# Two attention chunks per window: one set of scores in six PSUM banks, and whole output and query groups taking turns in two

## The chip, the cores and the metric

The kernel runs on one core of one Trainium2 chip. The metric is the device time of one execution in microseconds; three runs of the kernel before gave 1732.31, 1732.99 and 1734.68, a median of 1732.99.

The engines are named as the profile names them: PE is TensorE (matmuls; PEld is its weight loads), DVE is VectorE, ACT is ScalarE, POOL is GpSimd, and SP is SyncE, which issues nearly all DMAs here. Each engine works through its own list of instructions in order. [...]

## The reference, cut to what matters

Thirty-two batches of 512 query rows of 640 numbers attend to 77 context rows with 20 heads of 32 numbers. Only the text part of the original block is there, since the context has 77 rows and no more.

```
q = x @ to_q_w;  k = ctx @ to_k_w;  v = ctx @ to_v_w          # 640 wide, heads of 32
p = softmax(q k^T / sqrt(32))                                  # per head: 512 x 77
out = merge_heads(p v) @ to_out_w + to_out_b + x               # 32 x 512 x 640, float32
```

Everything is float32. Products that need more precision than one pass gives are made of a high and a low part in three passes, `(0,0), (0,1), (1,0)` of weights and data.

## The kernel before, in words

A first stage, which the change leaves alone, computes keys and values of all batches from the context and stores them in DRAM. It ends at about 250 us. The main loop then goes through 160 chunks: chunk n is one fifth of batch n // 5, that is 128 columns, or four heads (HPC = 4), of all 512 query rows, which make four tiles (NQ = 4) of 128.

For a chunk the steps are these:

- `queries(n)`: 15 matmuls (five parts of 128 input columns, three passes) into a PSUM bank of the kind `pq`. `copy_q` brings the bank to SBUF as `qt`.
- `scores(n)`: 16 matmuls of 77 columns, each recorded twice, one for each head and tile. The four heads sit in four row groups of TensorE and write four banks of the kind `sc`.
- `maxima(n)`: DVE takes the negative row maximum of each head's four tiles at once. `exps(n, i)`: ACT computes the exponentials of head i in four instructions, each with its sum, into `pn` (two buffers, by n mod 2).
- `normalize(n)`: DVE's reciprocal and POOL's multiplication in place. `transpose_p(n)`: DVE transposes 32x32 blocks of `pn` into `z` (two buffers).
- `move_p(n)`: four DMAs bring `z` into a `raw` buffer, of which there are two, with the keys on the partitions.
- `values(n)`: four matmuls (eight records) of `raw` and the batch's values into a bank of the kind `pa`. `high_a` (ACT) and `low_a` (DVE) split the result into a high and a low part, `at`. Ten such tiles live at a time.
- `group(b, c, ks)`: once all five chunks of batch b are there, the output projection of 128 columns, 15 matmuls into a bank `po`. `turn` (DVE) transposes it, and `add` (POOL) adds it to `ys[b]`, which holds x of the batch and gets the bias from `bias_of` (POOL). `store_y` writes it out with four DMAs.

The batch's x arrives through `load_x` (four DMAs, one for each quarter of the partitions), is transposed on DVE by `transpose_x` and split by `split_x` (ACT high, POOL low) into five `xt` tiles, of which seven live at a time. x and y buffers are taken in turn from three large ones (`natural`). So a `load_x` can have to wait until the stores from the buffer that it gets have landed.

The order of the work on each engine is written out by hand (`manual_schedule`): it is the order of the calls in `slot(n)`, lines 646 to 741, which runs once for each chunk. In the steady part, TensorE's order in a slot is: scores of n, nine matmuls of an output group, the 15 queries of n + 1, and the other six of the group. In every second slot the values of chunks n - 3 and n - 2 follow. DMAs on SP go out in the order of the code as well, and each issue first waits until its buffer is free and its data is there.

The last batch is handled in `end()`, where the output projection has rows on the partitions (`project`, `finish`).

## Time and profile before

| | |
|---|---|
| Median of three runs | 1732.99 us |
| The profiled execution's own time | 1730.84 us |
| Its span, first to last instruction | 1728.6 us |
| Granted TensorE clock, mean | 0.998 |
| PE busy | 1720.0 us, 100% |
| ACT busy | 1129.0 us, 65% |
| POOL busy | 987.1 us, 57% |
| DVE busy | 974.6 us, 56% |
| DMA bytes moved | 306.50 MB, 177 GB/s in the mean |

The page gives the busy time of each engine, the chain of work that ended last, and the costliest groups of instructions with their line, count and mean length. Other views of the same trace give the instructions of a stretch in order of time (start, length, line, and the idle time ahead of it with what ended it), the busy share of every engine in a stretch with the granted TensorE clock (1.00 is full speed) and the DMA engines' busy share, and for DMAs the time from the issue to the landing. `PE sc L455` is TensorE working on the tile `sc` in line 455. Times of a row are microseconds from the start of the span.

### The profile page before, as it was taken

Reading aid. Unit: us, or ns where it says so; the run is one execution under the profiler, and the core shown is the slowest. Engines: PE = TensorE matmul, PEld = TensorE weight load, DVE = VectorE, ACT = ScalarE, POOL = GpSimd, SP = SyncE. Lnnn points to the kernel's source line nnn. Section 1 sums busy time; section 2 is a strip of 40 time slices with the busy share of each in tenths; the row PEclk is TensorE's granted clock in tenths of the full one; section 3 lists DMA queues with packets and bytes.
Section 4 is the critical chain, followed back from the end, with each engine's and each line's share of the span. In section 5 each row is a group of like instructions: output and inputs, shape, how many; then the busy total and the mean of one; then the engine's idle time right before and its main releaser. Section 6 shows DMA issues by size and latency. Waiting matters only on the chain.

```text
span 1728.6 us, 36822 instructions
## 1 busy us (share of the span) xinstructions
PE 1720.0 (100%) x12460; PEld 1313.9 (76%) x12460; DVE 974.6 (56%) x1559; ACT 1129.0 (65%) x5698; POOL 987.1 (57%) x663
## 2 busy tenths in 40 slices
PE   9999999999999999999999999999999999999999
PEld 7888898677777777777777777777777777777777
DVE  5342235656666566665665666656666566665653
ACT  3131126777777777777777777777777777777771
POOL 1000026666666666666666666666666666666665
PEclk9999999999999999999999999999999999999999
DMA  9847565969888878887888888888878787888775
GB/s 186 163 88 183 115 134 146 214 152 207 177 190 176 189 177 192 189 197 176 192 191 175 193 184 184 184 182 185 195 174 200 166 196 179 192 176 189 176 169 160
DMA packets 363851, 306.50 MB, mean 177 GB/s; under 512 B 88784, under 2 KB 292112, under 8 KB 363664
## 3 DMA queue, kind: packets, MB, share of 16 engines
q1 hardware_dynamic: 360864, 296.61, 77.9%
q0 software_dynamic: 2704, 7.38, 1.4%
q8 instruction: 99, 1.62, 0.4%
q14 instruction: 88, 0.72, 0.1%
q10 hardware_dynamic: 96, 0.16, 0.0%
HBM read 120.36 MB, written 57.88 MB: 103 GB/s over the span
## 4 chain that ended last, share of the span: by engine, by line
PE 96%; DMA 2%; DVE 1%; SPq 1%; issue 0%; ACT 0%; POOL 0%; DVEq 0%; POOLq 0%; ACTq 0%
PE po L568 32%; PE pq L433 31%; PE sc L455 10%; PE pa L515 8%; PE pv L182 7%; PE pk L182 7%; DMA raw<-z 1%; PE po L600 1%; DMA wraw<-in_L_xattn_to_k_w_dram 1%; SPq L99 0%; DVE z L496 0%; DMA cs<-in_ctx_dram 0%; SPq L149 0%; DVE wk_s L90 0%; ACT wk_s L89 0%
## 5 line engine op out<-in xcount | busy, mean ns | idle before, releaser
L477 ACT ACTIVATE pn<-sc,nm 128x77 f32<-128x77 f32 x2560 | 788.6, 364 | 229.7 <-DVE nm L467 228.0
L489 POOL TENSOR_TENSOR pn<-pn,rs 128x1232 f32<-128x1232 f32 x160 | 363.4, 2271 | 478.8 <-DVE rs L487 474.1
L477 ACT ACTIVATION_READ_ACCUMULATOR pn<-sc,nm 128x1 f32 x2560 | 627.2, 245 | 0.0
L568 PE MATMUL po<-at,wo_s 128*128 128x512 f32 x2325 | 598.7, 398 | 0.0
L433 PE MATMUL pq<-xt,wq_s 128*128 128x512 f32 x2355 | 562.7, 390 | 0.0
L433 PEld LDWEIGHTS pq<-xt,wq_s 128*128 128x128 f32 x2355 | 442.3, 188 | 93.6
L568 PEld LDWEIGHTS po<-at,wo_s 128*128 128x128 f32 x2325 | 424.4, 188 | 97.6 <-DVE ot L578 0.8
L467 DVE TENSOR_REDUCE nm<-sc 128x4 f32<-128x308 f32 x640 | 261.1, 470 | 72.1 <-PE sc L455 72.1
L496 DVE STREAM_TRANSPOSE z<-pn 128x1536 f32<-128x1536 f32 x160 | 282.7, 1767 | 4.9 <-DMA raw<-z 3.0
L455 PEld LDWEIGHTS sc<-kb,qt 32*128 32x128 f32 x5120 | 158.1, 187 | 97.8 <-ACT at L529 63.7
L259 POOL TENSOR_TENSOR xt<-xs,xt 128x512 fp32r<-128x512 f32 x157 | 197.8, 1285 | 35.8 <-ACT xt L258 35.8
L578 DVE STREAM_TRANSPOSE ot<-po 128x512 f32<-128x512 f32 x155 | 111.1, 716 | 184.2 <-PE po L568 184.2
L582 POOL TENSOR_TENSOR xs<-xs,ot 128x512 f32<-128x512 f32 x155 | 200.2, 1292 | 2.3 <-DVE ot L578 2.1
L549 POOL TENSOR_TENSOR xs<-xs,bias_y 128x640 f32<-128x640 f32 x124 | 193.0, 1567 | 7.3
L455 PE MATMUL sc<-kb,qt 32*128 32x77 f32 x5120 | 181.8, 278 | 2.2 <-DVE qt L442 2.2
L529 ACT CAST at<-pa 128x512 fp32r<-128x512 f32 x160 | 94.3, 589 | 134.6 <-PE pa L515 134.6
L487 DVE RECIPROCAL rs<-sm 128x16 f32<-128x16 f32 x160 | 40.4, 252 | 219.6 <-ACT pn L477 219.6
L515 PE MATMUL pa<-raw,vb 96*32 96x512 f32 x1280 | 154.9, 599 | 1.3 <-DMA raw<-z 0.9
L534 DVE TENSOR_TENSOR at<-pa,at 128x512 fp32r<-128x512 f32 x160 | 109.6, 685 | 79.1 <-ACT at L529 79.1
L182 PE MATMUL pv<-ct,wv_s 128*128 128x512 f32 (+1 forms) x600 | 134.2, 382 | 0.0
L182 PE MATMUL pk<-ct,wk_s 128*128 128x512 f32 (+1 forms) x600 | 133.8, 382 | 0.3 <-ACT wk_s L89 0.2
L182 PEld LDWEIGHTS pk<-ct,wk_s 128*128 128x128 f32 x600 | 112.1, 188 | 20.2 <-ACT wk_s L89 0.8
(44 smaller groups left out, 698.2 us busy)
## 6 DMA issues: line engine op xcount, KB each, us to landing
raw<-z SPq DMA_DIRECT2D x640, 192.0 KB, 4.1
xs<-in_x_dram SPq DMA_DIRECT2D x256, 320.0 KB, 6.3
out_dram<-xs SPq DMA_DIRECT2D x127, 320.0 KB, 5.0
vb<-v_dram SPq DMA_DIRECT2D x32, 240.0 KB, 6.3
kb<-k_dram SPq DMA_DIRECT2D x32, 192.5 KB, 6.4
cs<-in_ctx_dram SPq DMA_DIRECT2D x12, 512.0 KB, 9.3
k_dram<-ks POOLq DMA_DIRECT2D x20, 256.0 KB, 2.5
v_dram<-vs SPq DMA_DIRECT2D x80, 64.0 KB, 2.3
```

The costliest lines, as they stand in the source:

```text
L182: nc.tensor.matmul(held[j][:, :gn], w[:, k, a, :], cts[g, k][:, c, :gn], start=(k == 0 and n == 0), stop=(k == NK - 1 and n == 2),)
L259: low.tensor_tensor(parts[1], src, parts[0].bitcast(F32), ALU.subtract)
L433: nc.tensor.matmul(pqs[n], wq_s[:, k, a, j * P : (j + 1) * P], xts[b, k][:, c, :], start=(k == 0 and m == 0), stop=(k == NC_ - 1 and m == 2),)
L455: nc.tensor.matmul(sc[:, t, :NKEY], qt[r, t * P : (t + 1) * P], kbs[b % 2][r, j, :], start=True, stop=True, tile_position=(i * HD, 0),)
L467: nc.vector.tensor_reduce(nms[n][:, i], sc[:, :, :NKEY], AX.X, ALU.max, negate=True)
L477: nc.scalar.activation(pnb[n % 2][:, at, :NKEY], sc[:, t, :NKEY], AF.Exp, bias=nms[n][:, i, t : t + 1], accum_out=sms[n][:, at : at + 1],)
L489: nc.gpsimd.tensor_tensor(pf, pf, rs.unsqueeze(2).to_broadcast([P, NQ * HPC, NKEY]), ALU.mult)
L496: nc.vector.transpose(z.rearrange("p c h t j -> p (h t) c j"), pn.rearrange("p a (c i) -> p a c i", i=Q),)
L515: nc.tensor.matmul(pas[n][i * HD : (i + 1) * HD, :].rearrange("p (a q) -> p a q", q=P), vb[:, i, :], raw[:, :, i, :], start=True, stop=Tru ...
L549: nc.gpsimd.tensor_tensor(part, part, biases[1].unsqueeze(1).to_broadcast([P, 4, U]), ALU.add)
L568: nc.tensor.matmul(pos[b, c], wos[0][:, k, a, c * P : (c + 1) * P], ats[b * NC_ + k][:, d, :], start=(k == 0 and m == 0), stop=(k == NC_ - ...
L582: nc.gpsimd.tensor_tensor(part, part, ots.pop((b, c)).rearrange("p (a i) -> p a i", i=Q), ALU.add)
```

## The change

From chunk 8 on, the loop over slots is replaced by a loop over windows of two chunks, n and n + 1, with n even. The work is the same, and its order changes:

- The values of chunks n - 4 and n - 3 come first and go to the banks `po` and `pq`, which output groups and queries use in turn afterwards.
- `scores_of_two` computes the scores of both chunks in one run of 64 records into six banks, the four of kind `sc` and both of kind `pa`. A head's own bank takes six tiles of 80 columns (four of chunk n, two of n + 1), and each of the two other banks takes the remaining two tiles of two heads. Maxima are taken over six tiles for each head, and over two in the shared banks.
- After the scores come a whole output group (15 matmuls), the queries of n + 2, another whole output group, and the queries of n + 3. `qt` has two buffers now. One copy of a window is ACT's, the other DVE's.
- `move_p(n - 2)` and `move_p(n - 1)` are issued in window n, and other DMAs of the window stand between them: with w = n mod 10 these are values, keys, two quarters of x and four of y for w = 0; values and four quarters of x for w = 4; keys and four of y for w = 6; four stores of y and two quarters of x for w = 8. For w = 2 four stores follow the second move.
- Bias additions, x splits and x transposes are dealt out to windows by w.
- In the fill (chunks 0 to 7) chunk 6 joins those whose probability transpose stands behind the query copy, and slot 7 computes the queries of chunks 8 and 9. In the end, two more output groups of the last but one batch are computed inside the last window (`closing`).

```diff
+    def scores_of_two(n):
+        banks = [bank("sc") for _ in range(HPC)] + [bank("pa") for _ in range(2)]
+        views = [
+            sc[:, : s * W].rearrange("p (s k) -> p s k", s=s)[:, :, :NKEY]
+            for sc, s in zip(banks, (6, 6, 6, 6, 4, 4))
+        ]
...
+        last = [(n + 1, 2), (n + 1, 3)]
+        rest = [(n, t) for t in range(NQ)] + [(n + 1, 0), (n + 1, 1)]
+        for step in range(2 * NQ):
+            for i in range(HPC):
+                m, t = (rest + last if i % 2 else last + rest)[step]
+                score(scs[m, i, t], m, i, t)
+            if step == 1:
+                for i in (0, 2):
+                    maxima_of(shared[i], i, 6)
+        return views, shared
...
+    def window(n):
+        w, b = n % 10, n // 10 * 2
+        first, ahead = n == FIRST, n + 2 < N
+        taken = (n - 3,) if first else (n - 4, n - 3)
+        early, later = (divmod(n - FIRST + i, NC_) for i in range(2))
+        for m in taken:
+            values(m, "pq" if m == n - 3 else "po")
+        for m in taken:
+            high_a(m)
+        while held:
+            low_a(held.pop())
+        normalize(n - 1)
+        for m in taken[:-1]:
+            low_a(m)
+        views, shared = scores_of_two(n)
+        low_a(n - 3)
+        for i in range(3):
+            maxima_of(views[i], i)
+        transpose_p(n - 1)
+        maxima_of(views[3], 3)
+        if not first:
+            move_p(n - 2)
+        if w == 0:
+            load_values(b)
+            load_keys(b + 1)
+            load_x(b + 1, (2, 3))
+            load_y(b - 1, range(4))
+        if w == 4:
+            load_values(b + 1)
+            if b + 2 < B:
+                load_x(b + 2)
+        if w == 6:
+            if b + 2 < B:
+                load_keys(b + 2)
+            load_y(b, range(4))
+        if w == 8:
+            if b:
+                store_y(b - 1, range(4))
+            if b + 3 < B:
+                load_x(b + 3, (0, 1))
...
+        for i in range(HPC):
+            exps(n, i)
+        group(*early, range(NC_))
+        turn(*early)
+        for i in (1, 3):
+            maxima_of(shared[i], i, 6)
+        add(*early)
+        move_p(n - 1)
+        if w == 2 and b > 1:
+            store_y(b - 2, range(4))
+        if ahead:
+            queries(n + 2)
+        normalize(n)
+        for i in (0, 2):
+            exps(n + 1, i, range(2, NQ))
+        if ahead:
+            copy_q(n + 2)
...
+        transpose_p(n)
+        for i in (1, 3):
+            exps(n + 1, i, range(2, NQ))
+        for i in (1, 3, 0, 2):
...
+            exps(n + 1, i, range(2))
...
+        if ahead:
+            group(*later, range(NC_))
+            turn(*later)
+            add(*later)
+            queries(n + 3)
+            copy_q(n + 3, nc.vector.tensor_copy)
...
-    for n in range(LATE, N):
+    for n in range(LATE, FIRST):
         slot(n)
+    for n in range(FIRST, N, 2):
+        window(n)
     end()
```

More of the change, by code (lines that the diff above doesn't have):

```diff
@@ L390 @@
     late = []
-    raws, ats, sms, pqs, pas, xrs, pos, scs, nms = ({} for _ in range(9))
+    raws, ats, sms, pqs, pas, xrs, pos, scs = ({} for _ in range(8))
     main.tile([P, HPC * NQ], F32, name="align")
@@ L402 @@
         pnb.append(pn)
-    qt = main.tile([P, S], F32, name="qt")
+    qts = [main.tile([P, S], F32, name="qt0")]
+    nmt = main.tile([P, 2 * HPC * NQ], F32, name="nm")
     ZSHAPE, U = [P, KBLK, HPC, NQ, Q], C // 4
     zs = [main.tile(ZSHAPE, F32, name="z0")]
-    biases = []
+    biases, nms, W, FIRST = [], {}, 80, 8
     def load_bias():
@@ L426, in load_values, with bank, queries @@
         )
-    def queries(n):
+    def bank(tag):
+        pool, bufs = (ps, {"sc": 4, "pq": 1}[tag]) if tag in ("sc", "pq") else (late[1], {"po": 1, "pa": 2}[tag])
+        return pool.tile([P, S], F32, tag=tag, name=tag, bufs=bufs)
+    def queries(n, tag="pq"):
         b, j = divmod(n, NC_)
-        pqs[n] = ps.tile([P, S], F32, tag="pq", name="pq", bufs=1)
+        pqs[n] = bank(tag)
         for k in range(NC_):
@@ L439, in queries, with qt_of @@
                 )
+    def qt_of(n):
+        return qts[n % 2 if n >= FIRST else 0]
     def copy_q(n, copy=nc.scalar.copy):
-        copy(qt, pqs.pop(n))
-    def scores(n):
-        b, j = divmod(n, NC_)
-        scs[n] = [
-            late[1].tile([P, NQ, P], F32, tag=LENT[n][i], name="sc", bufs=1 + (LENT[n][i] == "pa"))
-            if i in LENT.get(n, ())
-            else ps.tile([P, NQ, P], F32, tag="sc", name="sc", bufs=4)
-            for i in range(HPC)
-        ]
-        for t in range(NQ):
-            for i, sc in enumerate(scs[n]):
-                r = slice(i * HD, (i + 1) * HD)
-                nc.tensor.matmul(
-                    sc[:, t, :NKEY],
-                    qt[r, t * P : (t + 1) * P],
-                    kbs[b % 2][r, j, :],
-                    start=True,
-                    stop=True,
-                    tile_position=(i * HD, 0),
-                )
@@ L464, in maxima, with score @@
-    def maxima(n):
-        nms[n] = main.tile([P, HPC, NQ], F32, tag="nm", name="nm", bufs=2)
-        for i, sc in enumerate(scs[n]):
-            nc.vector.tensor_reduce(
-                nms[n][:, i], sc[:, :, :NKEY], AX.X, ALU.max, negate=True
-            )
-    def exps(n, i):
-        if i == 0:
+        copy(qt_of(n), pqs.pop(n))
+    def score(out, n, i, t):
+        b, j = divmod(n, NC_)
+        r = slice(i * HD, (i + 1) * HD)
+        nc.tensor.matmul(
+            out,
+            qt_of(n)[r, t * P : (t + 1) * P],
+            kbs[b % 2][r, j, :],
+            start=True,
+            stop=True,
+            tile_position=(i * HD, 0),
+        )
@@ new lines, in scores, with maxima @@
+    def scores(n):
+        banks = [bank(LENT.get(n, {}).get(i, "sc")) for i in range(HPC)]
+        views = [sc.rearrange("p (t k) -> p t k", t=NQ)[:, :, :NKEY] for sc in banks]
+        for t in range(NQ):
+            for i in range(HPC):
+                scs[n, i, t] = views[i][:, t]
+                score(views[i][:, t], n, i, t)
+        return views
+    def maxima(n, views):
+        for i in range(HPC):
+            nm = nmt[:, (n % 2 * HPC + i) * NQ : (n % 2 * HPC + i + 1) * NQ]
+            nc.vector.tensor_reduce(nm, views[i], AX.X, ALU.max, negate=True)
+            for t in range(NQ):
+                nms[n, i, t] = nm[:, t : t + 1]
@@ new lines, in scores_of_two @@
+    def scores_of_two(n):
[3 more added lines that the diff above has]
+            for sc, s in zip(banks, (6, 6, 6, 6, 4, 4))
+        ]
+        shared = {}
+        for i in range(HPC):
+            shared[i] = views[HPC + i // 2][:, i % 2 * 2 : i % 2 * 2 + 2]
+            for t in range(NQ):
+                scs[n, i, t] = views[i][:, t]
+                scs[n + 1, i, t] = views[i][:, NQ + t] if t < 2 else shared[i][:, t - 2]
+                for m in range(2):
+                    at = i * 2 * NQ + m * NQ + t
+                    nms[n + m, i, t] = nmt[:, at : at + 1]
+        last = [(n + 1, 2), (n + 1, 3)]
+        rest = [(n, t) for t in range(NQ)] + [(n + 1, 0), (n + 1, 1)]
+        for step in range(2 * NQ):
+            for i in range(HPC):
+                m, t = (rest + last if i % 2 else last + rest)[step]
[4 more added lines that the diff above has]
+        return views, shared
@@ L473, in exps, with maxima_of @@
+    def maxima_of(view, i, t0=0):
+        nm = nmt[:, i * 2 * NQ + t0 : i * 2 * NQ + (8 if t0 else 6)]
+        nc.vector.tensor_reduce(nm, view, AX.X, ALU.max, negate=True)
+    def exps(n, i, ts=range(NQ)):
+        if n not in sms:
             sms[n] = main.tile([P, NQ * HPC], F32, tag="sm", name="sm", bufs=2)
-        sc = scs[n][i]
-        for t in range(NQ):
+        for t in ts:
             at = i * NQ + t
@@ L478, in exps @@
                 pnb[n % 2][:, at, :NKEY],
-                sc[:, t, :NKEY],
+                scs.pop((n, i, t)),
                 AF.Exp,
-                bias=nms[n][:, i, t : t + 1],
+                bias=nms.pop((n, i, t)),
                 accum_out=sms[n][:, at : at + 1],
@@ L508, in move_p, with values @@
             )
-    def values(n):
+    def values(n, tag="pa"):
         b, j = divmod(n, NC_)
         raw, vb = raws.pop(n), vbs[b % 2][:, j]
-        pas[n] = late[1].tile([P, S], F32, tag="pa", name="pa", bufs=2)
+        pas[n] = bank(tag)
         for i in range(HPC):
@@ L556, in store_y @@
             nc.sync.dma_start(dst[q], ys[b][q * Q : (q + 1) * Q])
-    def bank(tag):
-        pool, bufs = (ps, {"sc": 4, "pq": 1}[tag]) if tag in ("sc", "pq") else (late[1], {"po": 1, "pa": 2}[tag])
-        return pool.tile([P, S], F32, tag=tag, name="po", bufs=bufs)
     def group(b, c, ks, tag="po"):
@@ L617, in finish, with take @@
             nc.sync.dma_start(out[last, rows, :], xr)
-    LATE = 2
-    LAG = 3
-    PAIRED = 8
-    takes = {n + LAG: (n,) for n in range(PAIRED - LAG)}
-    takes.update({n: (n - 3, n - 2) for n in range(PAIRED, N, 2)})
-    GROUP = {3: (1, 0), 4: (1, 1), 0: (2, 2), 1: (2, 3), 2: (2, 4)}
-    LOAD_X = {4: (2, (0, 1)), 0: (1, (2, 3))}
-    LOAD_Y = {1: (0, 1), 2: (2, 3)}
-    BIAS = {4: (1, (0, 1)), 0: (2, (2,)), 1: (2, (3,))}
-    STORE_Y = {3: range(4)}
-    TRANSPOSE_X = {1: (0, 1), 2: (2, 3)}
+    LATE, LAG = 2, 3
     EARLY_X = {4: 0, 6: 1}
-    SPLIT_X = {2: (0, 1), 3: (2, 3, 4)}
-    LENT = {3: {0: "po", 1: "pa"}, 4: {2: "po", 3: "pa"}, 6: {2: "po", 3: "pa"}, 8: {3: "pa"}}
-    held = []
+    LENT = {3: {0: "po", 1: "pa"}, 4: {2: "po", 3: "pa"}, 6: {2: "po", 3: "pa"}}
     WO = {1: (0, 1, 2), 4: (3,), 5: (4,)}
-    wos = []
-    def take(m):
-        values(m)
+    held, wos = [], []
+    def take(m, tag="pa"):
+        values(m, tag)
         high_a(m)
@@ L647, in slot @@
         b, j = divmod(n, NC_)
-        ahead, more = n + 1 < N, b + 1 < B
-        og, oc = b - GROUP[j][0], GROUP[j][1]
-        filling = n < NC_ + 2
-        copied = n in (3, 4, 5)
-        xsplits = (SPLIT_X if b else {0: (2,), 1: (3,), 2: (4,)}).get(j, ()) if more else ()
-        turns = TRANSPOSE_X.get(j, ()) if more and b > 1 else ()
-        taken = takes.get(n, ())
-        paired = n >= PAIRED and len(taken) > 0
-        scores(n)
-        if len(held) > 1:
-            for m in held:
-                high_a(m)
-            low_a(held.pop(0))
-        maxima(n)
+        copied, last = 3 <= n <= 6, n == FIRST - 1
+        views = scores(n)
+        maxima(n, views)
         while held:
             low_a(held.pop())
-        if n and filling and not copied:
+        if n and not copied and not last:
             transpose_p(n - 1)
@@ L667, in slot @@
             nc.sync.dma_start(wos[0][:, k].bitcast(F32), wo_dram[:, k].bitcast(F32))
-        if j == 0 and more:
+        if j == 0:
             load_keys(b + 1)
@@ L673, in slot @@
             load_x(2)
-        if j in LOAD_X and n > NC_ + 2 and b + LOAD_X[j][0] < B:
-            load_x(b + LOAD_X[j][0], LOAD_X[j][1])
-        if j in LOAD_Y and 0 < b < B:
-            load_y(b - 1, LOAD_Y[j])
-        if j in BIAS and b >= BIAS[j][0]:
-            for i in BIAS[j][1]:
-                bias_of(b - BIAS[j][0], i)
-        if og >= 0:
-            group(og, oc, range(3))
+        if n >= NC_ + 1:
+            load_y(0, ((0, 1), (2, 3))[n - NC_ - 1])
         for i in range(2):
             exps(n, i)
-        if not filling:
+        if last:
             transpose_p(n - 1)
-        if n >= LATE and n != PAIRED - 1 and not paired and not copied:
+        if n >= LATE and not last and not copied:
             move_p(n - 1)
-        if j in STORE_Y and b > 1:
-            store_y(b - 2, STORE_Y[j])
-        if not filling:
-            for i in turns:
-                transpose_x(b + 1, i)
         if len(beside) > 1:
             context_values(LAST, beside[1], psv)
-        if ahead:
-            queries(n + 1)
-        if filling or n == PAIRED - 1:
-            copy_q(n + 1, nc.vector.tensor_copy)
+        queries(n + 1)
+        copy_q(n + 1, nc.vector.tensor_copy)
         if copied:
@@ L702, in slot @@
             move_p(n - 1)
-        if not paired:
-            for m in taken:
-                values(m)
+        if n >= LAG:
+            values(n - LAG)
+        if last:
+            qts.append(late[0].tile([P, S], F32, name="qt1"))
+            queries(n + 2, "po")
+            copy_q(n + 2, nc.vector.tensor_copy)
         for i in range(2, HPC):
             exps(n, i)
-        normalize(n)
+        if not last:
+            normalize(n)
         if n == 1:
@@ L713, in slot @@
             context_values(LAST, beside[0], psv)
-        if not filling and n != PAIRED - 1 and ahead:
-            copy_q(n + 1)
-        if not paired:
-            for m in taken:
-                high_a(m)
-        if og >= 0:
-            group(og, oc, range(3, NC_))
-            turn(og, oc)
-        for m in taken:
-            if paired:
-                values(m)
-                held.append(m)
-            elif n < PAIRED:
-                held.append(m)
-            else:
-                low_a(m)
+        if n >= LAG:
+            high_a(n - LAG)
+            held.append(n - LAG)
         if n in EARLY_X:
@@ L733, in slot @@
             load_bias()
-        for c in xsplits if n != PAIRED - 1 else ():
-            split_x(b + 1, c)
-        if n == PAIRED - 1:
+        if n < 3:
+            split_x(1, n + 2)
+        if last:
             move_p(n - 1)
-        if og >= 0:
-            add(og, oc)
-        if paired:
-            move_p(n - 1)
-    def end():
+    BIAS = {0: (2, (1, 2, 3)), 4: (1, (0, 1)), 6: (1, (2, 3)), 8: (0, (0,))}
+    def window(n):
[38 more added lines that the diff above has]
+                load_x(b + 3, (0, 1))
+            if b + 2 < B:
+                for c in range(2, NC_):
+                    split_x(b + 2, c)
+        if w == 2:
+            for c in range(2):
+                split_x(b + 1, c)
+        for i in range(HPC):
+            exps(n, i)
[9 more added lines that the diff above has]
+            queries(n + 2)
+        normalize(n)
+        for i in (0, 2):
+            exps(n + 1, i, range(2, NQ))
+        if ahead:
+            copy_q(n + 2)
+        if w == 2:
+            for c in range(2, NC_):
+                split_x(b + 1, c)
+        if w in (0, 6) and b + w // 6 + 1 < B:
+            for i in range(NQ):
+                transpose_x(b + w // 6 + 1, i)
+        transpose_p(n)
+        for i in (1, 3):
+            exps(n + 1, i, range(2, NQ))
+        for i in (1, 3, 0, 2):
+            if i == 0 and w == 6 and b + 2 < B:
+                for c in range(2):
+                    split_x(b + 2, c)
+            if i == 0 and not ahead:
+                closing(n)
+            exps(n + 1, i, range(2))
+        if w in BIAS and b >= BIAS[w][0]:
+            for i in BIAS[w][1]:
+                bias_of(b - BIAS[w][0], i)
+        if ahead:
[4 more added lines that the diff above has]
+            copy_q(n + 3, nc.vector.tensor_copy)
@@ L746, in end, with closing @@
+    def closing(n):
         last = B - 1
@@ L748, in end @@
             load_residual(t)
-        take(N - 3)
-        group(last - 1, 2, range(NC_), "pq")
-        turn(last - 1, 2)
-        bias_of(last - 1, 2)
-        add(last - 1, 2)
-        transpose_p(N - 1)
-        move_p(N - 1)
-        group(last - 1, 3, range(NC_))
-        turn(last - 1, 3)
-        bias_of(last - 1, 3)
-        add(last - 1, 3)
-        take(N - 2)
-        group(last - 1, 4, range(NC_), "pq")
-        turn(last - 1, 4)
-        add(last - 1, 4)
+        for c, tag in ((1, "pq"), (2, "po")):
+            group(last - 1, c, range(NC_), tag)
+            turn(last - 1, c)
+            add(last - 1, c)
+        values(n - 2, "pq")
+        high_a(n - 2)
+    def end():
+        last = B - 1
+        low_a(N - 4)
+        move_p(N - 2)
+        normalize(N - 1)
+        take(N - 3, "po")
+        for c, tag in ((3, "pq"), (4, "po")):
+            bias_of(last - 1, c - 2)
+            group(last - 1, c, range(NC_), tag)
+            turn(last - 1, c)
+            if c == 3:
+                transpose_p(N - 1)
+                move_p(N - 1)
+            add(last - 1, c)
+        bias_of(last - 1, 3)
         store_y(last - 1, range(4))
@@ L766, in end, with begin @@
             add_bias(t)
-        def begin(i):
+        def begin(i, ks=range(4)):
             t, h = divmod(i, 2)
-            pos[t, h] = bank(("sc", "sc", "sc", "sc", "po", "pq", "pa", "pa")[i])
-            for k in range(4):
+            if 0 in ks:
+                pos[t, h] = bank(("sc", "sc", "sc", "sc", "po", "pq", "pa", "pa")[i])
+            for k in ks:
                 project(t, h, k)
@@ L777, in close @@
                 finish(t, h)
+        take(N - 2)
         for i in range(4):
-            begin(i)
+            begin(i, range(3))
+        for i in range(4):
+            begin(i, (3,))
         take(N - 1)
```

## The prediction

> **What bounds the kernel now.** I read the page first (busy shares, then the chain of waits), then the chain in one stretch of the steady part, then Sync's DMA issues there, and last the start of the main loop, where TensorE does wait.

> ```profile
> PE 1720.0 (100%) x12460; PEld 1313.9 (76%) x12460; DVE 974.6 (56%) x1559; ACT 1129.0 (65%) x5698; POOL 987.1 (57%) x663
> PE 96%; DMA 2%; DVE 1%; SPq 1%; issue 0%; ACT 0%; POOL 0%; DVEq 0%; POOLq 0%; ACTq 0%
> ```

> TensorE is the bound: it is busy for the whole span and carries 96% of the chain, while the other engines have a third of their time free. The chain in one stretch (start, length, block):

> ```profile
> 874.04 1.85 PE pa L515 x16
> 875.89 1.06 PE sc L455 x32
> 876.95 2.27 PE po L568 x9
> 879.22 3.40 PE pq L433 x15
> 882.62 1.36 PE po L568 x6
> 883.98 1.06 PE sc L455 x32
> 885.04 2.29 PE po L568 x9
> 887.34 3.41 PE pq L433 x15
> 890.75 1.36 PE po L568 x6
> 892.11 1.85 PE pa L515 x16
> ```

> Two chunks take 892.11 - 874.04 = 18.07 us without a gap. A plain matmul costs 3.40 / 15 = 0.227 us; nine output matmuls behind scores cost 2.27, not 2.04: each way out of the scores costs 0.23. TensorE's rows cut off at two moments show what the scores themselves cost:

> ```profile
> 875.82 0.35 PE L455 MATMUL sc<-kb,qt 32*128 32x77 f32 x4
> 875.82 1.02 PE L455 MATMUL sc<-kb,qt 32*128 32x77 f32 x28
> ```

> 24 more records, six rounds of four heads, take 0.67 us: 0.112 a round. Eight rounds are 0.90 of the 1.06, so a set of scores pays 0.16 once.

> **The tensor work of a window.** The change runs values of two chunks, 64 score records, then output group, query group, output group, query group, 15 matmuls each. No matmul is added or removed. Values 1.85; scores 1.06 + 8 x 0.112 = 1.95; output group behind them 2.27 + 1.36 = 3.63; the other three groups 3.40 + 3.41 + 3.41. The sum is 17.65 against 18.07: 0.41 gained, by one set entry and one way out less. There are 76 windows; the last has no queries and counts with the end, so 75 x 0.41 = 31 us.

> **DVE, ACT and PSUM.** The six-slot maxima and the four shared ones replace eight of four slots, over the same scores. Exponentials keep their number and ACT gives one of two query copies to DVE, which had 44% of the span free. Six banks are held from scores to exponentials, so values, groups and queries take turns in two: each first matmul waits for a copy or turn. The tightest is the values of n-3 in the bank that the last query group left:

> ```profile
> 289.16 0.69 DVE L442 COPY qt<-pq 128x512 f32<-128x512 f32 x1 [0.31 <-PE pq L433]
> 289.90 1.13 PE L455 MATMUL sc<-kb,qt 32*128 32x77 f32 x32 [0.79 <-DVE qt L442]
> ```

> TensorE went on 0.05 after that copy's end and 0.74 after its start. The values of n-4 go first for half of 1.85, some 0.9, so the copy is just covered: 0 taken, and if it began 0.3 later, 0.3 a window. The lows wait for the highs (ACT) in the same way under 1.95 of scores. Also 0. Bias adds, x splits and x transposes keep their number and come in bunches: in w=0 and w=6 four x transposes stand on DVE ahead of the second probability transpose and of the turn that frees the bank for the next values. DVE's free 44% of a window are 7.8 us, mostly in its second half where they fall: 0; without that cover the next values would wait for the turn.

> **The DMAs, where I see the loss.** Before and after, a chunk's probabilities go through four `raw<-z` DMAs, and a `raw` buffer (two) is free once the values of two chunks earlier have read it. Now both buffers are freed at a window's start, and both refills must land before the next window's start, with the window's other DMAs between them on Sync's queue. In windows with n mod 10 = 8 (write that w=8) it issues move n-2, four stores of y, two loads of x into the buffer that these stores empty, move n-1. In the kernel before, the same twelve issues follow each other every ten chunks, 14 times; the same list as of w=0 (two moves, keys, values, six quarters of x and y) runs right behind:

> ```profile
> 917.09 2.50 SPq L505 DMA_DIRECT2D raw<-z  x4
> 919.69 4.61 SPq L556 DMA_DIRECT2D out_dram<-xs  x4
> 927.94 0.86 SPq L244 DMA_DIRECT2D xs<-in_x_dram  x2
> 929.27 3.04 SPq L505 DMA_DIRECT2D raw<-z  x4
> SPq L244 <- DMA out_dram<-xs: 46.8, 16, 4.2
> L505 SPq DMA_DIRECT2D raw<-z x4: 577/674/983, 929.3 to 931.3; - x4
> DMA to landing us min/median/max: 6.1/6.4/6.7
> 1007.39 2.50 SPq L505 DMA_DIRECT2D raw<-z  x4
> L505 SPq DMA_DIRECT2D raw<-z x4: 577/597/1217, 1019.6 to 1021.5; - x4
> DMA to landing us min/median/max: 4.9/5.1/5.3
> 1549.23 2.50 SPq L505 DMA_DIRECT2D raw<-z  x4
> L505 SPq DMA_DIRECT2D raw<-z x4: 571/584/1243, 1561.4 to 1563.6; - x4
> DMA to landing us min/median/max: 6.9/7.2/7.7
> 927.90:948.60 20.70, 20.70 (x178) 14.45 (x176) 12.79 (x20) 13.36 (x70) 15.21 (x10) 1.00 0.97 195
> ```

> The load stood behind the stores until 927.94, and the second move landed at 931.3 + 6.7 = 938.0: 20.9 us after the first was issued. At 1007.39 it is 19.3, at 1549.23 it is 22.0. Before, that wait lies ahead of the moment at which a buffer is freed and costs nothing; in a window it lies between the moves. When does the first move start, and when must the second be there?

> ```profile
> 892.04 1.92 PE L515 MATMUL pa<-raw,vb 96*32 96x512 f32 x16
> 893.16 2.56 SPq L505 DMA_DIRECT2D raw<-z  x4
> ```

> It starts 1.12 behind the first value matmul. The values of n-1 start half a value block, 0.9, into the next window: 17.65 + 0.9 = 18.5. With 20.2 (little follows the second move here, so under the middle row) it lands at 21.3: TensorE waits 2.8 us, 1.9 to 4.6 by the rows. It is behind in order, so nothing else runs. 14 windows have stores and loads (n = 18 to 148). For w=0 the last row above has the DMA engines 0.97 busy for 20.7 us with that window's list, so its second move lands at 1.12 + 20.7 = 21.8, 3.3 late; behind a stalled w=8 its deadline has moved by as much and I add nothing, so only n = 10 pays. w=4 and w=6 carry two quarters less and no store: 0 to 0.3 each, 3 us in all. w=2 stores last: 0.

> **What a wait does to the clock.** At the start of the loop:

> ```profile
> 306.92 1.13 PE L455 MATMUL sc<-kb,qt 32*128 32x77 f32 x32
> 311.98 1.06 PE L515 MATMUL pa<-raw,vb 96*32 96x512 f32 x8 [0.30 <-DMA raw<-z]
> 314.46 2.00 PE L455 MATMUL sc<-kb,qt 32*128 32x77 f32 x32 [1.42 <-DVE qt L442]
> 322.25 1.07 PE L515 MATMUL pa<-raw,vb 96*32 96x512 f32 x8
> 332.95 1.06 PE L515 MATMUL pa<-raw,vb 96*32 96x512 f32 x8 [0.55 <-DMA raw<-z]
> 310.97:314.38 3.41, 1.77 (x12) 0.43 (x10) 2.42 (x3) 3.41 (x23) 0.28 (x1) 1.00 1.10 254
> 314.38:321.21 6.83, 6.75 (x43) 5.62 (x44) 3.00 (x7) 5.06 (x30) 3.49 (x2) 0.50 1.15 188
> 331.45:334.86 3.41, 2.86 (x48) 1.14 (x45) 1.40 (x2) 1.94 (x4) 3.41 (x3) 1.00 0.36 81
> ```

> After a 3.41 us stretch with TensorE busy for 1.77, the granted clock was 0.50 for 6.83 us. Scores and 15 query matmuls then took 322.25 - 314.46 = 7.79, against 311.98 - 0.30 - 306.92 = 4.76 before: 3.0 lost. A stretch with 0.55 idle lost nothing. A wait of 2.8 passes 1.64 idle in one such stretch in most phases; I take 9 in 10, 2.7 us. [...]

> **Fill and end.** The fill moves a transpose of probabilities behind the query copy, so the 1.42 above may go, with its 3.0; but chunk 9's queries stand behind the values of chunk 4, whose move is then waited for. Taken 0, between -4 and +4. The end keeps its matmuls with one change of kind less: 0, -1 to +1.

> **Sum.** Against the profiled execution, 1730.84 (span 1728.6): -31 + 14 x (2.8 + 2.7) = +77, + 6 for n = 10 (3.3 + 2.7), + 3: 1786. The median of the runs stands 2.15 above the profiled one: 1788.

> **Rivals.**
> [...]
> 2. The moves are in time: faster. The second move would have to land within 18.5 - 1.1 = 17.4 of the first's issue, with fewer DMAs around it. Then 1733 - 31 = 1702. Against: the quickest of the quoted sequences takes 19.3. It decides where each of 15 places loses under 31 / 15 = 2.1.
> 3. One more wait on top: GpSimd. In w=6 it has two splits, two bias adds and an add behind the second normalization; if they push the next normalization, transpose and fourth maxima past ACT's first twelve exponentials, some 1.5 us in 16 windows: 1788 + 24 = 1812. For it: 57% busy in one queue; against: the fourth maxima have room.

> **How the numbers follow.** My case 0.55 (its own range 1762 to 1812), the first rival 0.2 (1735 to 1762), the second 0.15, the third 0.1. The range 1731 to 1814 leaves out the second and little of the third. About 0.2% (3.5 us) is what a measurement here tells from no change: faster 0.15, within it 0.03 (the low edge of the first rival), slower 0.82.

> **What would show it.** Right: TensorE rows of values with a wait on DMA `raw<-z` of 2 to 4 us at the second value block of each w=0, a clock of 0.50 behind most, Sync's wait of the x load on the stores as before, 17.65 us for undisturbed windows. Wrong: no such waits and 17.65 throughout (rival 2), waits at full clock (rival 1), waits of scores or values on DVE in every window (my covers fail), or 18 us windows (no gain in the scores).

## The result, and the profile after

The changed kernel takes 1783.42 us in the median (1780.97 to 1791.44), against 1732.65 for the kernel before, run beside it. The ratio is 1.0302, with a 95% interval of 1.0265 to 1.0338: 3.0% slower. Forecast were 1788 and a range of 1731 to 1814.

The page of the profiled execution (1791.44 us, the slowest of its runs) has these counterparts to the lines shown of before: the busy shares, the granted clock in 40 slices, and the chain.

```profile
span 1789.6 us, 36879 instructions
PE 1740.6 (97%) x12460; PEld 1342.1 (75%) x12460; DVE 1012.5 (57%) x1635; ACT 1077.6 (60%) x5622; POOL 989.7 (55%) x663
PEclk9999999899898999998999998999999899999899
PE 81%; DMA 11%; SPq 6%; issue 1%; POOL 1%; DVE 0%; ACT 0%; DVEq 0%; ACTq 0%
```

TensorE has the same 12460 records as before, but 17% of the chain is now DMAs and Sync's queue, where it was 3%; and the clock row, which is 9 at full speed, has an 8 in seven of its 40 slices. The list of what TensorE waited for (us in total, times, longest) names the tile at once. The list of Sync's own waits follows it:

```profile
PE pq L554 <- DMA raw<-z: 35.1, 17, 3.2
PE pa L554 <- DMA raw<-z: 2.7, 2, 1.4
```

```profile
SPq L544 <- PE po L554: 288.6, 75, 5.1
SPq L244 <- DMA out_dram<-xs: 52.7, 21, 4.5
```

`pq L554` is the second value block of a window. One such place is the end of a window with n mod 10 = 8 and the start of the one with 0, here n = 18 and n = 20. First comes TensorE in order of time (single score records left out):

```profile
427.89 1.06 PE L554 MATMUL po<-raw,vb 96*32 96x512 f32 x8
428.77 1.04 PE L554 MATMUL pq<-raw,vb 96*32 96x512 f32 x8
...
431.70 3.70 PE L603 MATMUL po<-at,wo_s 128*128 128x512 f32 x15
435.23 3.56 PE L438 MATMUL pq<-xt,wq_s 128*128 128x512 f32 x15
438.63 3.56 PE L603 MATMUL po<-at,wo_s 128*128 128x512 f32 x15
442.03 3.56 PE L438 MATMUL pq<-xt,wq_s 128*128 128x512 f32 x15
445.52 1.07 PE L554 MATMUL po<-raw,vb 96*32 96x512 f32 x8
448.79 1.90 PE L554 MATMUL pq<-raw,vb 96*32 96x512 f32 x8 [2.20 <-DMA raw<-z]
...
454.26 5.97 PE L603 MATMUL po<-at,wo_s 128*128 128x512 f32 x15
```

The window lasts 445.52 - 427.89 = 17.63 us; 17.65 was forecast. Then the second value block stands 2.20 us for `raw<-z`, and behind that wait the output group takes 5.97 in place of 3.70. Next come Sync's issues in that window (the last row joins its second move with the first move of the next window), and in a second view the four DMAs of its second move (issue ns and times, landing in us):

```profile
429.01 3.30 SPq L544 DMA_DIRECT2D raw<-z  x4
432.41 4.30 SPq L595 DMA_DIRECT2D out_dram<-xs  x4
440.50 0.85 SPq L244 DMA_DIRECT2D xs<-in_x_dram  x2
441.46 7.82 SPq L544 DMA_DIRECT2D raw<-z  x8
```

```profile
L544 SPq DMA_DIRECT2D raw<-z x4: 577/597/1362, 441.5 to 443.4; - x4
DMA to landing us min/median/max: 5.2/5.3/5.3
```

The first move goes out 1.12 behind the first value matmul, as assumed. The four stores are issued by 436.7; the x load waits for them until 440.50, and the move behind it is issued only from 441.46 to 443.4 and lands at 443.4 + 5.3 = 448.7, when the values go on. That is 19.7 us after the first move (20.2 forecast). The last view is the clock, in the stretch with the wait and behind it, and then at the place with n = 70 (length, busy time of PE, PEld, DVE, ACT, POOL, clock, DMA share, GB/s):

```profile
445.47:448.88 3.41, 1.21 (x13) 0.28 (x16) 1.54 (x3) 0.58 (x1) 2.27 (x1) 1.00 0.94 225
448.88:459.12 10.24, 10.24 (x84) 7.38 (x83) 5.08 (x8) 4.62 (x28) 0.00 (x0) 0.50 1.05 226
916.51:919.92 3.41, 1.91 (x16) 0.39 (x17) 1.54 (x3) 0.58 (x1) 1.97 (x1) 1.00 0.75 182
919.92:926.75 6.83, 6.83 (x91) 5.47 (x84) 5.37 (x9) 4.08 (x24) 0.30 (x1) 1.00 0.94 218
```

With 1.21 us busy out of 3.41 the clock was halved for 10.24 us; with 1.91 busy, at n = 70, it was not. The table has all windows of the steady part, each from its first value matmul to the next window's. A value block is called late by the time that it starts behind the 0.88 us of an undisturbed window; the idle time in the rows is about 0.2 shorter, since the rows of neighbouring blocks overlap.

| n mod 10 | windows | length, median (range) | what is in the excess |
|---|---|---|---|
| 4, 6, 8 | 44 | 17.62 (17.62 to 17.63) | nothing |
| 0 | 15 | 22.97 (18.40 to 25.31) | the second values 1.7 to 3.4 us late in 14 of them, a halved clock behind 11 |
| 2 | 15 | 17.61; four of 18.84 to 23.04 | n = 12: wait and clock, 5.4; n = 52, 72, 142: late by 1.2 to 1.4, where the clock had stayed full at n = 50, 70, 140 |

The account of the two profiled spans, 1789.6 - 1728.6 = +61.0: 75 x (17.62 - 18.06) = -33; over 17.62, the 14 stalled windows with n mod 10 = 0 add up to +76, those with 2 to +9, n = 10 to +1; the fill is about 6 longer. The sum is +59.

### The profile page after: what moved, and what is told of

Same layout as the page of the kernel before. It is cut to its first block, busy times and chain, and to the rows that moved or that the text cites. A ratio compares the mean times of both kernels' runs of the same rounds, so it can differ in the third digit from the quotient of the medians.

```text
span 1789.6 us, 36879 instructions
## 1 busy us (share of the span) xinstructions
PE 1740.6 (97%) x12460; PEld 1342.1 (75%) x12460; DVE 1012.5 (57%) x1635; ACT 1077.6 (60%) x5622; POOL 989.7 (55%) x663
## 4 chain that ended last, share of the span: by engine, by line
PE 81%; DMA 11%; SPq 6%; issue 1%; POOL 1%; DVE 0%; ACT 0%; DVEq 0%; ACTq 0%
PE po L603 26%; PE pq L438 24%; PE pv L182 7%; PE pk L182 7%; DMA raw<-z 6%; PE sc L455 6%; PE pq L554 4%; PE po L554 3%; DMA out_dram<-xs 3%; PE pa L455 3%; SPq L544 3%; SPq L595 2%; DMA wraw<-in_L_xattn_to_k_w_dram 1%; SPq L244 1%; DMA wo_s<-wo_dram 1%
## 5 line engine op out<-in xcount | busy, mean ns | idle before, releaser
L516 ACT ACTIVATE pn<-sc,nm 128x77 f32<-128x77 f32 x1928 | 597.4, 364 | 154.1 <-DVE nm L509 127.9
L603 PE MATMUL po<-at,wo_s 128*128 128x512 f32 x2295 | 578.1, 405 | 0.0
L603 PEld LDWEIGHTS po<-at,wo_s 128*128 128x128 f32 x2295 | 442.1, 195 | 98.1
L516 ACT ACTIVATION_READ_ACCUMULATOR pn<-sc,nm 128x1 f32 x1928 | 472.0, 246 | 0.0
L516 ACT ACTIVATE pn<-pa,nm 128x77 f32<-128x77 f32 x620 | 198.1, 366 | 9.3 <-DVE nm L509 9.1
L509 DVE TENSOR_REDUCE nm<-sc 128x6 f32<-128x462 f32 x304 | 177.1, 624 | 30.9 <-PE pa L455 30.9
L455 PE MATMUL sc<-kb,qt 32*128 32x77 f32 x3856 | 183.2, 295 | 0.0
L568 ACT CAST at<-po 128x512 fp32r<-128x512 f32 x76 | 44.5, 585 | 229.2 <-PE po L554 229.2
L455 PEld LDWEIGHTS sc<-kb,qt 32*128 32x128 f32 x3856 | 170.0, 209 | 4.2 <-issue 3.1
L450 DVE COPY qt<-pq 128x512 f32<-128x512 f32 x83 | 57.3, 691 | 192.3 <-PE pq L438 192.3
L516 ACT ACTIVATION_READ_ACCUMULATOR pn<-pa,nm 128x1 f32 x620 | 151.3, 247 | 0.0
L455 PEld LDWEIGHTS pa<-kb,qt 32*128 32x128 f32 x1240 | 94.5, 208 | 70.3 <-ACT at L568 47.8
```

The lines of the kernel that those rows point to most:

```text
L455: nc.tensor.matmul(out, qt_of(n)[r, t * P : (t + 1) * P], kbs[b % 2][r, j, :], start=True, stop=True, tile_position=(i * HD, 0),)
L509: nc.vector.tensor_reduce(nm, view, AX.X, ALU.max, negate=True)
L516: nc.scalar.activation(pnb[n % 2][:, at, :NKEY], scs.pop((n, i, t)), AF.Exp, bias=nms.pop((n, i, t)), accum_out=sms[n][:, at : at + 1],)
L603: nc.tensor.matmul(pos[b, c], wos[0][:, k, a, c * P : (c + 1) * P], ats[b * NC_ + k][:, d, :], start=(k == 0 and m == 0), stop=(k == NC_ - ...
```

## The experiments

All are edits of the changed kernel.

**The x load behind the second move.** This takes the wait of the load on the stores out from between the moves of windows with n mod 10 = 8.

```
@@ w == 8
-            if b + 3 < B:
-                load_x(b + 3, (0, 1))
@@ behind move_p(n - 1)
+        if w == 8 and b + 3 < B:
+            load_x(b + 3, (0, 1))
```

> Edit: in w=8 the two loads of x go out behind the second move instead of ahead of it. Theory (the second move stands on Sync's queue behind stores, the load that waits for them, and the load's own traffic): the wait of values for the DMA raw<-z at the start of the w=0 windows, 2.1 us in the median, goes, and so do their half-clock stretches. The loads then run into the w=0 window, whose own list took the DMA engines 20.7 us in the kernel before, so that window's second move is 3 to 5 us late and the wait comes back at the start of w=2, with the clock: 1775 to 1800 us in all, as much as before or little less. Rival (the store's landing is the whole cause): no waits anywhere, near 1705 us. Rival (the moves are late by themselves, in whatever order): waits stay at w=0.

Measured: 1813.44 (1810.39 to 1816.54), ratio 1.0472 (1.0453 to 1.0490). TensorE in order of time, with Sync's second move of the window with n = 18 as the last row, and then TensorE's waits:

```profile
445.55 1.06 PE L554 MATMUL po<-raw,vb 96*32 96x512 f32 x8
446.43 1.04 PE L554 MATMUL pq<-raw,vb 96*32 96x512 f32 x8
...
463.58 1.07 PE L554 MATMUL po<-raw,vb 96*32 96x512 f32 x8 [0.33 <-DVE ot L613]
466.71 1.68 PE L554 MATMUL pq<-raw,vb 96*32 96x512 f32 x8 [2.06 <-DMA raw<-z]
437.41 3.73 SPq L544 DMA_DIRECT2D raw<-z  x4
```

```profile
PE pq L554 <- DMA raw<-z: 31.6, 14, 5.0
PE po L554 <- DVE ot L613: 11.2, 10, 2.4
```

The place that waited (445.55) waits no more: the load of x ahead of it was what made that move late. The move now goes out at 437.41 and not at 441.46; most of the difference is the load's wait for the stores, 3.8 us from 436.71 to 440.50, and the edit does not part this wait from the load's own traffic. But the waits come back one window on, at the 14 windows with n mod 10 = 2 from n = 22. (The view's 14 counts otherwise: its longest, 5.0, is in the fill, one is that of n = 12, and two of the 14 are listed under DVE, for `at`.) In the window of n = 20 the second move is issued from 456.64 on, only 10.0 us behind the first, but its DMAs take up to 8.3 us to land where those of n = 18 took up to 4.0, and the DMA engines are 0.98 busy from the first issue to the landing, 19.8 us. So one late list is replaced by another, and here no issue is held up: the window with n mod 10 = 0 has no room for what was pushed into it. A new wait came as well, on DVE's turn `ot`. In the profiled execution the clock was halved for 10.24 us at each of the 14 places, and was 0.955 in the mean against 0.968. With n = 12 that is 154 us at half speed, where the same count in the changed kernel's windows is 102; half the difference, 26 us, is about what the profiled spans differ by (1814.8 and 1789.6), and it is why the result lies above the expectation.

**The y load behind the second move.** Only in windows with n mod 10 = 0.

```
@@ w == 0
-            load_y(b - 1, range(4))
@@ behind move_p(n - 1)
+        if w == 0:
+            load_y(b - 1, range(4))
```

> Edit: in w=0 the four loads of y go out behind the second move. Theory: waits at w=0 are made in w=8 and stay (14 of about 2.1 us with a half clock behind most); the four waits at the start of w=2 (n = 12 and three where the clock had stayed full) go, which were 9 us in all: about 1775 us. Rival (w=0's load of the DMA engines makes the waits at w=0 too): these shrink as well, below 1750 us.

Measured: 1775.36 in the median of five executions (1755.22 to 1783.37). The ratio on record is 1.0280 (1.0254 to 1.0306), but two of the five, at 1755.22 and 1770.27, are only 1.4% and 2.2% above the kernel before, so that interval is narrower than the spread. The waits at n mod 10 = 0 stay, since they belong to the list of 8, and all windows with 2 are at 17.61 to 17.63. The profiled execution was the fastest: its 14 waits halved the clock in seven places, where the changed kernel's halved it in 11, and its clock was 0.983 in the mean against 0.968. So nearly the same waits cost more or less; what decides it is not shown.

**Both loads behind.**

> Both edits: x loads of w=8 and y loads of w=0 behind the second move. Theory: no wait for raw<-z in the steady part, clock 1.00 there, every window 17.62 us; the profiled execution of the changed kernel lost 86.8 us in windows longer than that, so about 1783 - 80 = 1703 us (1697 to 1712), faster than the kernel before. Rival (the DMA engines have not the time for these transfers in 17.6 us windows whatever the order): waits move to other windows and the time stays above 1740 us.

Measured: 1718.12 (1717.41 to 1721.60), ratio 0.9925 (0.9910 to 0.9940): faster than the kernel before. Neither edit alone removes the loss, both together do, and no value block of the steady part waits for a move any more. But 15 us are missing against the expectation. The waits of TensorE, then DVE in order of time in a window with n mod 10 = 0:

```profile
PE po L554 <- DVE ot L613: 12.0, 12, 2.4
```

```profile
357.21 3.02 DVE L248 STREAM_TRANSPOSE xs<-xs 128x640 f32<-128x640 f32 x4 [3.05 <-DMA xs<-in_x_dram]
360.15 1.74 DVE L535 STREAM_TRANSPOSE z<-pn 128x1536 f32<-128x1536 f32 x1
361.81 0.67 DVE L613 STREAM_TRANSPOSE ot<-po 128x512 f32<-128x512 f32 x1
362.41 0.65 DVE L450 COPY qt<-pq 128x512 f32<-128x512 f32 x1
```

DVE ran nothing for 3.05 us while its four transposes of x waited for x quarters that land late; the probabilities and the turn that frees the values' bank stand behind them, at 360.15 and 361.81. Windows with n mod 10 = 0 take 18.49 in the median in place of 17.62, and two places lose the clock, at about 5 us each.

**All of x loaded behind the move of 8, nothing of x left in 0.** If that reading holds, x must land earlier:

```
@@ w == 0
-            load_values(b)
-            load_keys(b + 1)
-            load_x(b + 1, (2, 3))
-            load_y(b - 1, range(4))
@@ w == 8
-            if b + 3 < B:
-                load_x(b + 3, (0, 1))
@@ behind move_p(n - 1)
+        if w == 8 and b + 3 < B:
+            load_x(b + 3)
+        if w == 0:
+            load_values(b)
+            load_keys(b + 1)
+            load_y(b - 1, range(4))
```

> In w=8 all four quarters of the next x are loaded, behind the move of n-1; in w=0 values, keys and y are loaded behind the move of n-1, and no x is left there. If in the kernel with both loads moved the values of w=0 stood for DVE's turn because DVE's four x transposes stood for the late quarters of x (3.05 us at 357.21), they find x landed now: w=0 comes down from 18.49 (up to 20.08, two places 22.4) to about 17.62, w=2 stays at 17.61, no value waits on raw<-z in the steady part, clock 0.99 or above: about 1720 - 22 = 1698 (1692 to 1705). Rival, DVE's bunch of transposes itself is too long for w=0: the waits on ot at w=0 stay and the time stays at about 1718. Second rival, four quarters behind w=8's move push the first move of w=0: waits on raw<-z at w=0 or w=2 come back, 1730 or more.

Measured: 1702.76 (1698.90 to 1703.52), ratio 0.9822 (0.9809 to 0.9835). DVE in the same kind of window:

```profile
359.11 3.02 DVE L248 STREAM_TRANSPOSE xs<-xs 128x640 f32<-128x640 f32 x4
362.06 1.73 DVE L535 STREAM_TRANSPOSE z<-pn 128x1536 f32<-128x1536 f32 x1
363.72 0.67 DVE L613 STREAM_TRANSPOSE ot<-po 128x512 f32<-128x512 f32 x1
367.00 0.69 DVE L450 COPY qt<-pq 128x512 f32<-128x512 f32 x1 [2.60 <-PE pq L438]
```

The transposes wait for nothing, and DVE is ready 2.60 us before the next query group ends. Every one of the 74 windows is between 17.61 and 17.63. The edit also puts the values and keys of these windows behind their second move, so it is not a test of x alone; that the wait for x is gone is read from DVE's rows.

**The same, and y in the fill behind its last move.**

> The kernel above, and in the fill the four quarters of the first y are loaded behind the last move of the fill and not between moves. If the waits on raw<-z of 1.3 to 2.9 us in the fill come from these loads standing ahead of moves on Sync's queue, they shrink, and with them the halved clock there: 0 to 6 us less than the kernel above, 1692 to 1698. If they come from the moves being issued late (chunk 9's queries behind the values of chunk 4), the fill stays and the time is the same within 2 us.

Measured: 1696.84 (1695.17 to 1697.09), ratio 0.9794 (0.9780 to 0.9807). The page, and what is left of TensorE's waits for moves:

```profile
span 1695.0 us, 36834 instructions
PEclk9999999999999999999999999999999999999999
PE 96%; DMA 2%; DVE 1%; SPq 1%; ACT 0%; issue 0%; DVEq 0%; ACTq 0%
```

```profile
PE pa L554 <- DMA raw<-z: 2.1, 2, 1.4
```

In the kernel without this edit the fill's last values and the output group behind them were

```profile
329.31 1.06 PE L554 MATMUL pq<-raw,vb 96*32 96x512 f32 x8 [3.53 <-DMA raw<-z]
...
333.71 5.42 PE L603 MATMUL po<-at,wo_s 128*128 128x512 f32 x15
```

and with it

```profile
325.00 1.07 PE L554 MATMUL pq<-raw,vb 96*32 96x512 f32 x8
...
328.48 3.69 PE L603 MATMUL po<-at,wo_s 128*128 128x512 f32 x15
```

so the wait and the clock that it cost are gone (1.000 in the mean, and 0.998 without the edit). This version is 2.1% faster than the kernel before: the change of the tensor work is worth what its windows say, once DMAs that are needed later no longer stand ahead of the moves.

**Work in place of idle time.** To part the wait from the clock, matmuls whose results are overwritten are put ahead of the second value block, into its bank, in windows with n mod 10 = 0 from n = 20 on: nine (2.04 us), four (0.9) and two (0.45).

```
-    def values(n, tag="pa"):
+    def values(n, tag="pa", idle=0):
+        for _ in range(idle):
+            nc.tensor.matmul(pas[n], wq_s[:, 0, 0, :P], wq_s[:, 0, 0, :S], start=True, stop=True)
...
-            values(m, "pq" if m == n - 3 else "po")
+            values(m, "pq" if m == n - 3 else "po", 9 * (w == 0 and n > 10 and m == n - 3))
```

> Edit: nine extra matmuls, 2.04 us, into the bank of the second values between the two value blocks of the w=0 windows from n = 20 on; they are overwritten and only keep TensorE busy while it would wait. Theory (an idle stretch of about 2 us halves the clock for 7 to 10 us, which is the larger part of a w=0 window's 5.35 us): the wait shrinks to 0 to 1 us, the clock stays full in most places, a w=0 window falls from 23.0 to about 19.8 us, and where the clock stayed w=2 starts with a wait of 1 to 1.5 us: per place 5.35 becomes 2.2 + 1.2, in all about 1757 us (1745 to 1768), faster although work is added. Rival (windows behind a wait are slow because of the traffic or of other engines, not of the idle time): the extra matmuls add or leave the time, 1780 us or more.

> Four overwritten matmuls (0.9 us) in place of nine between the value blocks of w=0; their results are overwritten by the values. The second values still wait for the move, so each w=0 ends where it does with nine, but TensorE stands idle for about 2.2 - 0.9 = 1.3 us of it. If it is the idle time within one 3.41 us stretch that halves the clock, with the turn at about 1.6, nearly all places stay at full clock: 1752, as with nine (1748 to 1758), PEclk 0.99 or above. Rival, any wait after a long busy stretch halves it: the clock stays at 0.97 and the time at about 1783.

> Two overwritten matmuls (0.45 us): TensorE stands idle for about 1.75 us of each wait, on the turn. By the theory of idle time within one stretch about half of the places lose the clock: 1752 + 7 x 4 - 4 (no later waits at w=2 behind those) = 1765 to 1775, between the run without and the one with four. By the rival about 1783.

Measured:

| matmuls added at each of 14 places | median (range) | ratio (interval) |
|---|---|---|
| 0 | 1783.42 (1780.97 to 1791.44) | 1.0302 (1.0265 to 1.0338) |
| 2 | 1766.51 (1755.62 to 1776.77) | 1.0177 (1.0139 to 1.0215) |
| 4 | 1761.88 (1760.54 to 1767.64) | 1.0178 (1.0156 to 1.0199) |
| 9 | 1751.78 (1750.63 to 1756.08) | 1.0120 (1.0103 to 1.0137) |

With nine, and then with four, TensorE in order of time at one such place (the added matmuls are `L554`, and the values have moved to `L556`):

```profile
440.15 1.07 PE L556 MATMUL po<-raw,vb 96*32 96x512 f32 x8
441.14 2.34 PE L554 MATMUL pq<-wq_s 128*128 128x512 f32 x9
443.53 1.06 PE L556 MATMUL pq<-raw,vb 96*32 96x512 f32 x8
```

```profile
444.91 1.06 PE L556 MATMUL po<-raw,vb 96*32 96x512 f32 x8
445.90 1.20 PE L554 MATMUL pq<-wq_s 128*128 128x512 f32 x4
449.67 1.06 PE L556 MATMUL pq<-raw,vb 96*32 96x512 f32 x8 [2.57 <-DMA raw<-z]
```

With four, this place has the longest wait; the 13 others have idle times of 0.3 to 1.2. These are stretches of the run with four, with the columns as above:

```profile
445.29:448.70 3.41, 1.81 (x12) 0.67 (x4) 1.27 (x3) 0.59 (x1) 2.27 (x1) 1.00 1.06 250
1377.13:1380.54 3.41, 1.82 (x17) 0.34 (x16) 1.54 (x3) 0.59 (x1) 3.39 (x2) 1.00 0.46 112
1380.54:1387.37 6.83, 6.83 (x74) 5.56 (x71) 3.59 (x7) 3.33 (x14) 2.60 (x3) 0.50 0.35 87
```

The data come no sooner (with nine, the second values of these places are late by 2.6 in the mean, without by 2.3), and adding work that is thrown away makes the kernel 32 us faster: that part of the loss was the clock, which is 0.997 in the mean in place of 0.968. What is left with nine is the length of the waits, now filled, and smaller waits at n mod 10 = 2: 1752, inside the first rival's range for waits at full clock (1735 to 1762). The rival of the two smaller doses, that any wait halves the clock, falls: behind the wait of 2.57 us above, the values took 1.06, where at half clock they took 1.90 (448.79 in the changed kernel). Both doses lie between none and nine, but that four beats two is not shown: their ratios are the same and their ranges overlap. The dose of four lies above its 1758. Besides n = 12, which has no added work, its profiled execution lost the clock at n = 122 and n = 132, since where it stays full at n mod 10 = 0, nearly every next window waits again, late by 0.6 to 1.8 us. The idle time is no sharp edge: 1.60 us in the stretch at 445.29 left the clock full, 1.59 at 1377.13 halved it.

## Why the prediction was right

**Tensor work of a window: right.** 17.65 worked out, 17.62 measured. The output group behind the scores takes the 3.63 that was assumed (`441.26 3.63 PE po L603 x15` in the chain of the kernel with all of x behind the move; the row of 3.70 above overlaps its neighbours). The gain of 31 us is there in full: 75 windows at 17.62 in place of 18.06 are 33, and with the waits of the steady part removed the kernel stands at 1702.76, where the second rival's sum was 1702.

**DVE, ACT and PSUM at 0: right for the changed kernel.** The tight copy is just covered: it starts at 428.00 and the second values at 428.77. There were no waits on DVE in the 44 undisturbed windows. The condition named there ("without that cover the next values would wait for the turn") came true in experiments, when late x moved DVE's transposes: 12 us of waits, and about 10 more for the clock. My expectation for both loads moved missed it, as I had counted the landing of x as nobody's concern.

**The second move's lateness: right in place, count and cause.** The wait comes at the second values of n mod 10 = 0 from n = 20 to 150, 14 places, and n = 10's list is paid at n = 12. Its size was forecast at 2.8 and is 2.3 in the mean (1.7 to 3.4): the move landed 19.7 after the first in the place shown and not 20.2.

**The clock: right as a mechanism, mis-sized in both factors.** 9 in 10 places at 3.0 us were forecast, 2.7 in the mean. It was 11 of 14, and the 76 us of excess less 14 x 2.3 of waits leave 44, so 4.0 us each, 3.1 in the mean: at six of the 11 the clock was halved for 10.24 us and not for 6.83. Waits taken too long, a halving taken too often and its price taken too low offset each other: 14 places forecast at +77, measured +76. That the sum comes so close is luck; the halving is not: the clock fell to 0.50 behind 11 of the 14 waits, for 6.83 us behind a stretch with 1.66 us busy out of 3.41 (at 1479.71, n = 130) and for 10.24 behind one with 1.21 (at 445.47, n = 20), and it was 0.997 in the mean where nine matmuls filled the waits.

**The small terms.** n = 10's list: 6 forecast, 5.4 measured. n mod 10 = 4 and 6: 3 forecast, 0 measured. Not forecast in the sum: later waits at n = 52, 72, 142, 4 us, where a full clock at n mod 10 = 0 brings the next deadline forward, 1.2 to 1.4 a place. The end: 0, as taken. The fill: 0 taken, between -4 and +4; in the profiled execution about +6, through three waits of 1.3 to 2.9 us and the clock. The fill varies: of seven other profiles with the same fill, three had it at -1 to +2 (y behind, both behind, nine matmuls) and four at +4 to +7 (the x load behind, all of x behind, two and four matmuls). So its term was mostly too low. It may also be part of why the profiled execution stands 8 us above the median, where 2.15 had been added for the reverse; the other executions left no trace.

**The rivals.** First (waits at full clock, 1735 to 1762): 1752 was measured with nine added matmuls, which keep the clock at 0.997; by itself the kernel as changed lost the clock behind 11 of 14 waits. Second (moves in time): did not come by itself, but is what the kernel does when the loads are moved. Third (GpSimd): nothing of it in the trace; windows with 6 and 8 are at 17.63.

**Slips in the working.** Three leave the forecast as it is. The line of the sum reads as if the -31 were inside the +77; 14 x 5.5 alone is 77, and the total of 1786 has both. The rows quoted for the list of the kernel before are fourteen issues and not twelve. And there are 15 windows with n mod 10 = 6, not 16, which makes the third rival 1810 or 1811.

## What to carry to other kernels

When a change frees two buffers at once where it freed them in turn, list what stands between their refills on the issuing queue: a load that waits for stores to land, harmless before, can hold up the urgent transfer behind it (here it waited 3.8 us, and the move behind it left TensorE waiting 2.20), so put transfers with a deadline first and those without behind, and check who reads the latter and whether the next list has room for them. Here a wait of a little over 2 us on TensorE cost 2.2 us where the clock stayed full (n = 140) and 7.3 where it was halved (n = 20), so a wait must be priced with what runs after it. And a loss of 3% may sit on top of a real gain: undisturbed windows show it, and the order of a few DMAs can give it back.
